# A Mamba block and an FP4 feed-forward on one core: the first tiles of the feed-forward are loaded, quantized and scheduled in another order

## The chip, the core and the metric

The kernel runs on one core of a Trainium2 chip. Its engines are TensorE (PE, with its weight loads shown as PEld), VectorE (DVE), ScalarE (ACT), GpSimd (POOL) and SyncE (SP, which here issues the DMAs). Each engine takes its own instructions in order, and waits on semaphores for the others. The metric is the time of one execution on the device, in microseconds (us). All data are float32.

## What is computed

The input is x with 8192 rows of 512. The first half is a Mamba block; the second a gated feed-forward network (FFN) whose three products take inputs and weights rounded to FP4 in blocks of 16. Cut to what matters:

```python
def fp4_quant_dequant(x):               # along the last dim, BLOCK = 16
    xb = x.reshape(shape[:-1] + (shape[-1] // BLOCK, BLOCK))
    scale = jnp.maximum(jnp.max(jnp.abs(xb), -1, keepdims=True) / 6.0, 1e-12)
    xn = xb / scale
    idx = jnp.searchsorted(_MID, jnp.abs(xn))
    return (_GRID[idx] * jnp.sign(xn) * scale).reshape(shape)
...
gate = fp4_linear(x, w_gate); y = fp4_linear(x, w_up)
h = jax.nn.silu(gate) * y
return fp4_linear(h, w_down)
...
h = _layernorm(x) * (1 + ca) + sa
x = x + ga * mamba(h, ...)
h = _layernorm(x) * (1 + cb) + sb
return x + gb * ffn(h, w_gate, w_up, w_down)
```

The inner width of the FFN is 1408. ga and gb are gates of 512 values, worked out in the kernel from the conditioning vector; gb multiplies the FFN's result column by column.

## The kernel before, in words

The first half works through the 8192 rows in 16 chunks of 512 and writes x's update, gated, to `mo` in DRAM, one tensor per chunk. Its instructions stand in an order written out by hand (`TABLE`, under `tc.manual_schedule()`). Beside its first chunk it quantizes w_gate and w_up and stores them turned in DRAM (`wqs`), and it stores the rows cb+1, sb and gb in `rows`. Its last steps are: the last scan steps (L497) and product with C (L521) on DVE, sums through PE (L392), the gate `z` times y (L404, DVE), four transposes (L410) with copies on ACT (L417), and for each of the last four groups of 128 rows an output projection of eight matmuls (L423), copied from PSUM by ACT (L436, one PSUM buffer) and stored to `mo` (L437).

At `order.close()` the hand-written order ends. From there a scheduler orders the instructions of each engine by data and estimated cost; where it puts one is seen only in the built program. What stands in the code there, in this order: loads of `sb`, `cb1` and the quantized w_gate and w_up (`wg`, `wu`, six loads, L869); `normed` for tile 0 in a pool `hd`; and the last steps of the first half.

The FFN works through 64 tiles of 128 rows:

- `head(t)` calls `normed` (L871 on): it loads `x1` (from `mo`, L874) and `h2` (from x, L876), adds them on POOL (L877), takes the layer norm on DVE (L25 to L32, with a power on POOL, L31), multiplies by cb1 and adds sb on POOL (L879, L880), and quantizes to `xq`.
- `up(t)` transposes xq on PE (L913), copies it (ACT, L937), and in chunks of 512, 512 and 384 columns multiplies it by wg and wu (L945: `pg` and `pu`, two PSUM buffers each), takes silu on ACT (L950) and the product on DVE (L951) into `h`. Then it quantizes h, 1408 wide, to `hq`.
- `down(t)` transposes hq, copies it (ACT, L958), multiplies by `wd` (L962: 11 steps into `po2`), adds to x1 on DVE (L965) and stores the result.

Quantizing, in `_fp4_steps`, is one chain for any width: block maximum (L63, DVE), scale (L65), reciprocal (L67), division `xn` (L69, on the engine given as `first`), magnitude and a slope on ACT (L73, L75), four roundings on DVE (L79 to L82), and the scale put back on POOL (L87).

W_down is quantized in the first four passes, one group of 128 rows per pass, by `quantize_down`, with L69 on DVE; in the pass after, `turn_down` transposes it on PE (L913, shared PSUM buffers `ptp`, two of them), and DVE multiplies the result by gb while it copies it from PSUM (L924). No `down` can run before all of `wd` is there, so `up` runs ahead:

```python
late.append((t, xt, up(t, q)))
if t < NK:
    rows_d[t] = quantize_down(t)
if 0 < t <= NK:
    turn_down(t - 1, rows_d.pop(t - 1))
if t >= NK:
    for _ in range(min(2, len(late) - 1)):
        down(*late.pop(0))
```

NK is 4. Passes 4 to 6 do two down() each, later ones one, and one is left for the end.

Of the kernel before, what the change touches and what calls it, by code (L numbers as in the profile page):

```python
# [8 lines left out]
F32 = mybir.dt.float32  # L9
U32 = mybir.dt.uint32  # L10
AF = mybir.ActivationFunctionType
ALU = mybir.AluOpType
# [4 lines left out]
P = 128  # L17
# [24 lines left out]
    nc.vector.scalar_tensor_tensor(out, sgn, mul, mag, ALU.subtract, ALU.mult)  # L42


def _fp4_steps(nc, work, small, src, dst, n, slope0, first):

    nb = n // BLK
    blocks = lambda t: t.rearrange("p (b k) -> p b k", k=BLK)
    spread = lambda t: t.unsqueeze(2).to_broadcast([P, nb, BLK])
    magic = float(2**21 + 1)
    t = {}

    def scales():
        am = small.tile([P, nb], F32, tag="am", name="am")
        nc.vector.tensor_reduce(am, blocks(src), AX.X, ALU.max, apply_absolute_value=True)  # L63
        sc = t["sc"] = small.tile([P, nb], F32, tag="sc", name="sc")
        nc.vector.tensor_scalar(sc, am, 1.0 / 6.0, 1e-12, ALU.mult, ALU.max)  # L65
        rs = small.tile([P, nb], F32, tag="rs", name="rs")
        nc.vector.reciprocal(rs, sc)  # L67
        xn = t["xn"] = work.tile([P, n], F32, tag="xn", name="xn")
        first.tensor_tensor(blocks(xn), blocks(src), spread(rs), ALU.mult)  # L69

    def leads():
        a = t["a"] = work.tile([P, n], F32, tag="a", name="a")
        nc.scalar.activation(a, t["xn"], AF.Abs)  # L73
        e = t["e"] = work.tile([P, n], F32, tag="e", name="e")
        nc.scalar.activation(e, a, AF.Identity, bias=slope0, scale=2.2)  # L75

    def rounds():
        a, e, xn = t.pop("a"), t.pop("e"), t["xn"]
        nc.vector.scalar_tensor_tensor(e, a, 2.0, e, ALU.add, ALU.max)  # L79
        nc.vector.tensor_scalar(e.bitcast(U32), e.bitcast(U32), 0xFFE00000, None, ALU.bitwise_and)  # L80
        nc.vector.scalar_tensor_tensor(xn, e, magic, xn, ALU.mult, ALU.add)
        nc.vector.scalar_tensor_tensor(xn, e, -magic, xn, ALU.mult, ALU.add)  # L82

    def values():
        xn = t.pop("xn")
        to = xn if dst is None else dst
        nc.gpsimd.tensor_tensor(blocks(to), blocks(xn), spread(t.pop("sc")), ALU.mult)  # L87
        return to

    return scales, leads, rounds, values  # L90


def _fp4(*args):
    for step in _fp4_steps(*args):
        step()
# [3 lines left out]
def mamba_then_fp4_ffn(  # L99
# [18 lines left out]
    nc = tc.nc  # L118
    L, DM = x.shape
    DI = w_outT.shape[0]  # L120
    FF = w_gate.shape[0]
    NS = a_log.shape[2]
    RK = w_dtT.shape[0]
    NK = DM // P
    ND = DI // P
    NF = FF // P
# [10 lines left out]
    small = ctx.enter_context(tc.tile_pool(name="small", bufs=4))  # L137
# [7 lines left out]
    slope0 = glob.tile([P, 1], F32, tag="slope0", name="slope0")  # L145
    nc.gpsimd.memset(slope0, -1.72)
    sc = glob.tile([P, NK], F32, tag="silu_c", name="silu_c")
# [7 lines left out]
    rows = dram.tile([3, DM], F32, tag="rows", name="rows")  # L155


    with ExitStack() as ma:
# [697 lines left out]
                        run(slot, moment)  # L856

        order.close()
        wq = ctx.enter_context(tc.tile_pool(name="wq", bufs=1, side="right", **own))
        wg = wq.tile([P, NK, FF], F32, tag="wg", name="wg")  # L860
        wu = wq.tile([P, NK, FF], F32, tag="wu", name="wu")
# [2 lines left out]
        NCH = [(o, min(512, FF - o)) for o in range(0, FF, 512)]  # L864
        nc.sync.dma_start(sb, rows[0:1, :].partition_broadcast(P))
        nc.sync.dma_start(cb1, rows[1:2, :].partition_broadcast(P))
        for o, w in NCH:
            for t, key in ((wg, "g"), (wu, "u")):
                nc.sync.dma_start(t[:, :, o : o + w], wqs[key][:, :, o : o + w])  # L869

        def normed(t, io, work, small_work, dst):  # L871

            xt = io.tile([P, DM], F32, tag="x1", name=f"x1_{t}")
# [9 lines left out]
                step()  # L883
            return xt, values()


        hd = ctx.enter_context(tc.tile_pool(name="hd", bufs=1, side="right", **own))
        nxt = normed(0, hd, hd, hd, None)

        for slot in range(NSLOT, last + 1):  # L890
            run_all(slot)
# [2 lines left out]
    with ExitStack() as fa:  # L894
        wq2 = fa.enter_context(tc.tile_pool(name="wq2", bufs=1, **own))
        wd = wq2.tile([P, NF, DM], F32, tag="wd", name="wd")
        gb = wq2.tile([P, DM], F32, tag="gb", name="gb")
        nc.sync.dma_start(gb, rows[2:3, :].partition_broadcast(P))
        wide = fa.enter_context(tc.tile_pool(name="wide", bufs=2, **own))
        work = fa.enter_context(tc.tile_pool(name="fwork", bufs=2, **own))  # L900
        fsm = fa.enter_context(tc.tile_pool(name="fsm", bufs=3, **own))
        io = fa.enter_context(tc.tile_pool(name="fio", bufs=NK + 1, **own))
        pdn = fa.enter_context(tc.tile_pool(name="pdn", bufs=2, space=PSUM, **own))
        pgu = fa.enter_context(tc.tile_pool(name="pgu", bufs=2, space=PSUM, **own))
        ptp = fa.enter_context(tc.tile_pool(name="ptp", bufs=2, space=PSUM, **own))

        def transposed(src, nblk, put):

            for b0 in range(0, nblk, 4):
                nb = min(4, nblk - b0)  # L910
                pt = ptp.tile([P, 4, P], F32, tag="mm", name="pt")
                for b in range(nb):
                    nc.tensor.transpose(pt[:, b, :], src[:, (b0 + b) * P : (b0 + b + 1) * P], ident)  # L913
                put(b0, nb, pt)

        def quantize_down(r):
            raw = wide.tile([P, FF], F32, tag="wraw", name=f"wraw_{r}")
            nc.sync.dma_start(raw, w_down[r * P : (r + 1) * P, :])
            _fp4(nc, work, fsm, raw, raw, FF, slope0, nc.vector)
            return raw  # L920

        def turn_down(r, q):

            transposed(q, NF, lambda b0, nb, pt: nc.vector.tensor_tensor(  # L924
                wd[:, b0 : b0 + nb, r * P : (r + 1) * P], pt[:, :nb, :],
                gb[:, r * P : (r + 1) * P].unsqueeze(1).to_broadcast([P, nb, P]), ALU.mult))

        NT = L // P

        def head(t):  # L930
            q = work.tile([P, DM], F32, tag="xq", name=f"xq_{t}")
            return normed(t, io, work, fsm, q)

        def up(t, q):

            qT = work.tile([P, NK, P], F32, tag="xqT", name=f"xqT_{t}")
            transposed(q, NK, lambda b0, nb, pt: nc.scalar.activation(  # L937
                qT[:, b0 : b0 + nb, :], pt[:, :nb, :], AF.Copy))
            hb = wide.tile([P, FF], F32, tag="h", name=f"h_{t}")
            for o, w in NCH:  # L940
                pg = pgu.tile([P, 512], F32, tag="pg", name=f"pg_{t}_{o}")
                pu = pgu.tile([P, 512], F32, tag="pu", name=f"pu_{t}_{o}")
                for ps, wt in ((pg, wg), (pu, wu)):
                    for k in range(NK):
                        nc.tensor.matmul(  # L945
                            ps[:, :w], lhsT=qT[:, k, :], rhs=wt[:, k, o : o + w],
                            start=(k == 0), stop=(k == NK - 1),
                        )
                g = wide.tile([P, 512], F32, tag="g", name=f"g_{t}_{o}")
                nc.scalar.activation(g[:, :w], pg[:, :w], AF.Silu)  # L950
                nc.vector.tensor_tensor(hb[:, o : o + w], g[:, :w], pu[:, :w], ALU.mult)  # L951
            hq = wide.tile([P, FF], F32, tag="q", name=f"hq_{t}", bufs=NK + 1)
            _fp4(nc, work, fsm, hb, hq, FF, slope0, nc.vector)
            return hq

        def down(t, xt, hq):
            hT = wide.tile([P, NF, P], F32, tag="hqT", name=f"hqT_{t}")
            transposed(hq, NF, lambda b0, nb, pt: nc.scalar.activation(  # L958
                hT[:, b0 : b0 + nb, :], pt[:, :nb, :], AF.Copy))
            po = pdn.tile([P, DM], F32, tag="po", name=f"po2_{t}")  # L960
            for f in range(NF):
                nc.tensor.matmul(  # L962
                    po, lhsT=hT[:, f, :], rhs=wd[:, f, :], start=(f == 0), stop=(f == NF - 1)
                )
            nc.vector.tensor_tensor(xt, xt, po, ALU.add)  # L965
            nc.sync.dma_start(out[t * P : (t + 1) * P, :], xt)


        late, rows_d = [], {}
        for t in range(NT):  # L970
            xt, q = nxt
            if t + 1 < NT:
                nxt = head(t + 1)
            late.append((t, xt, up(t, q)))
            if t < NK:
                rows_d[t] = quantize_down(t)
            if 0 < t <= NK:
                turn_down(t - 1, rows_d.pop(t - 1))
            if t >= NK:
                for _ in range(min(2, len(late) - 1)):  # L980
                    down(*late.pop(0))
        for args in late:
            down(*args)


# [38 lines left out]
```

## Time and profile before

Three executions took 6126.43, 6127.5 and 6128.48 us (median 6127.5). The profiled one took 6128.15 us; its span, from the first instruction to the last, is 6126.4 us.

| engine | busy us | share of the span | busy, 4400 to 4430.5 us |
|---|---|---|---|
| PE | 5440.3 | 89% | 29.56 |
| DVE | 4928.0 | 80% | 18.47 |
| POOL | 4147.2 | 68% | 8.33 |
| ACT | 3092.8 | 50% | 7.26 |

The last column is one pass of the settled FFN. The first half ends, and the FFN begins, at about 4040 us of the span. How to read the profile: a group or a stretch says what an engine was doing; "idle before <-X" says how long it stood before an instruction, and what it waited for last. A wait counts against the time only if nothing else is late too. So times of a stage are compared with that stage's own rows, not with averages over the whole span. DVE or POOL being idle costs nothing by itself; PE being idle while it has most of the work does.

### The profile page before, as it was taken

To read this page: it belongs to the slowest core of one execution; us is meant where nothing else is said; L and a number is where in the kernel's file an instruction comes from. 1 tells how busy PE (TensorE), PEld (TensorE's weight loads), DVE (VectorE), ACT (ScalarE), POOL (GpSimd) and SP (SyncE) were. 2 spreads that over 40 slices of the span, in tenths; PEclk is the share of its full clock that TensorE was granted. 3 is DMA by queue.
4 is the path that set the end of the run, shared out by engine and by line. 5 is a ranking of instruction groups with operands and counts; after the bars stand their busy time and mean duration, and the time that the engine had idled before them with its cause. 6 is when DMAs were issued, how large, how long until landed. Compare 5 with 4: busy or idle time off the path is not lost.

```text
span 6126.4 us, 60004 instructions
## 1 busy us (share of the span) xinstructions
PE 5440.3 (89%) x20772; PEld 3253.4 (53%) x20772; DVE 4928.0 (80%) x5007; ACT 3092.8 (50%) x5708; POOL 4147.2 (68%) x2415
## 2 busy tenths in 40 slices
PE   7788888889888888898888888678999999999999
PEld 4555555555555555555555555534444444444444
DVE  6999899999999999999998989966566666666664
ACT  6576666676666666666666665522222222222222
POOL 4999999999999999999989999942222222222221
PEclk9899989889899999898998999888999999999999
DMA  5444444444444444444444444420000000000000
GB/s 179 158 148 148 145 149 150 147 147 146 149 153 144 150 146 148 150 149 150 149 145 148 149 144 149 153 96 24 26 26 25 26 26 26 26 26 23 26 24 14
DMA packets 220552, 659.78 MB, mean 108 GB/s; under 512 B 24371, under 2 KB 36787, under 8 KB 220246
## 3 DMA queue, kind: packets, MB, share of 16 engines
q1 hardware_dynamic: 220246, 655.94, 33.2%
q8 instruction: 163, 2.67, 0.2%
q14 instruction: 143, 1.17, 0.1%
HBM read 615.48 MB, written 40.38 MB: 107 GB/s over the span
## 4 chain that ended last, share of the span: by engine, by line
PE 34%; DVE 19%; ACT 8%; issue 2%; POOL 2%; DVEq 0%; POOLq 0%; DMA 0%; SPq 0%; ACTq 0%
PE pg L945 10%; PE po L962 10%; DVE da L497 10%; PE pu L945 9%; DVE hc L521 4%; ACT da L471 4%; DVE hp L497 3%; PE pt L913 1%; PE cv L296 1%; POOL db L461 1%; PE y L392 1%; ACT xqT L937 1%; ACT L347 1%; PE cv L268 1%; ACT hqT L958 1%
## 5 line engine op out<-in xcount | busy, mean ns | idle before, releaser
L461 POOL TENSOR_TENSOR db<-bc,du 128x1024 f32<-128x1024 f32 x1024 | 2398.0, 2362 | 49.2 <-DVE da L497 41.6
L497 DVE TENSOR_TENSOR_SCAN da<-da,state,db 128x512 f32<-128x512 f32 x1280 | 1645.1, 1285 | 97.4 <-ACT da L471 71.8
L471 ACT ACTIVATE da<-delta,na 128x512 f32<-128x512 f32 x2048 | 1410.6, 690 | 418.5 <-DVE hc L521 197.3
L87 POOL TENSOR_TENSOR hq<-xn,sc 128x1408 f32<-128x1408 f32 x64 | 189.2, 2957 | 1318.3 <-DVE xn L82 1318.3
L497 DVE TENSOR_TENSOR_SCAN hp<-da,state,db 128x512 f32<-128x512 f32 x768 | 941.2, 1267 | 152.1 <-PE y L392 58.5
L392 PE MATMUL y<-ident,hc 128*128 128x128 f32 x5120 | 774.9, 302 | 233.9 <-DVE hc L521 233.7
L513 POOL TENSOR_TENSOR hp<-hp,bc 128x1024 f32<-128x1024 f32 x384 | 904.8, 2356 | 30.8 <-POOL state L512 0.2
L392 PEld LDWEIGHTS y<-ident,hc 128*128 128x128 f32 x5120 | 659.8, 156 | 407.7 <-DVE hc L521 320.2
L521 DVE TENSOR_TENSOR hc<-da,bc 128x1024 f32<-128x1024 f32 x640 | 781.1, 1220 | 30.8 <-DVE da L497 0.9
L945 PE MATMUL pg<-wg,xqT 128*128 128x512 f32 (+1 forms) x1536 | 652.7, 568 | 44.0 <-ACT xqT L937 44.0
L945 PE MATMUL pu<-wu,xqT 128*128 128x512 f32 (+1 forms) x1536 | 635.9, 557 | 0.0
L962 PE MATMUL po<-wd,hqT 128*128 128x512 f32 x1408 | 616.5, 593 | 0.0
L950 ACT ACTIVATE g<-pg 128x512 f32<-128x512 f32 (+1 forms) x192 | 107.8, 561 | 956.9 <-PE pg L945 956.9
L268 PE MATMUL cv<-hT,w_in 128*128 128x512 f32 x1024 | 504.8, 639 | 46.5 <-ACT delta L347 43.2
L296 PE MATMUL cv<-raw,taps 128*128 128x512 f32 x1024 | 523.3, 659 | 6.7 <-ACT taps L282 6.7
L366 PE MATMUL pz<-w_in,hT 128*128 128x256 f32 x2048 | 495.1, 397 | 28.8 <-ACT delta L347 26.4
L945 PEld LDWEIGHTS pg<-wg,xqT 128*128 128x128 f32 x1536 | 290.5, 192 | 361.9 <-issue 250.8
L951 DVE TENSOR_TENSOR h<-g,pu 128x512 f32<-128x512 f32 (+1 forms) x192 | 123.4, 643 | 426.2 <-PE pu L945 421.3
L423 PE MATMUL po<-w_o,xc 128*128 128x512 f32 x1024 | 461.2, 594 | 2.8 <-ACT po L436 2.1
L945 PEld LDWEIGHTS pu<-wu,xqT 128*128 128x128 f32 x1536 | 291.8, 190 | 312.9 <-issue 244.3
L366 PEld LDWEIGHTS pz<-w_in,hT 128*128 128x128 f32 x2048 | 401.3, 201 | 91.7 <-ACT delta L347 32.3
L392 PE MATMUL y<-ident,hp 128*128 128x128 f32 x3072 | 433.6, 288 | 0.0
(118 smaller groups left out, 6347.3 us busy)
## 6 DMA issues: line engine op xcount, KB each, us to landing
bc<-bc SPq DMA_DIRECT2D x1024, 512.0 KB, 4.6
x<-in_x_dram SPq DMA_DIRECT2D x64, 256.0 KB, 4.9
mo<-po SPq DMA_DIRECT2D x64, 256.0 KB, 2.1
h<-in_x_dram SPq DMA_DIRECT2D x64, 256.0 KB, 2.7
x<-mo SPq DMA_DIRECT2D x64, 256.0 KB, 2.6
out_dram<-x SPq DMA_DIRECT2D x64, 256.0 KB, 2.0
w_in<-in_w_inT_dram SPq DMA_DIRECT2D x2, 2048.0 KB, 9.0
wm<-in_wmod_dram SPq DMA_DIRECT2D x8, 512.0 KB, 4.7
```

What stands on the lines that cost most here:

```text
L268: nc.tensor.matmul(ps, lhsT=w_in[:, f, o : o + P], rhs=hT[k][:, f, :], start=(f == 0), stop=(f == NK - 1),)
L296: nc.tensor.matmul(v, lhsT=taps[:, i, :], rhs=raw[:, i : i + T], start=(i == 0), stop=(i == 3))
L366: nc.tensor.matmul(pz[:, b, :], lhsT=hT[k][:, f, t0 : t0 + P], rhs=w_in[:, f, o : o + DH * P], start=(b == 0 and f == 0), stop=(f == NK - ...
L392: nc.tensor.matmul(y[:, j, i * P : (i + 1) * P], lhsT=src[:, j * P : (j + 1) * P], rhs=ident, start=start and j % 2 == 0, stop=stop, is_tr ...
L423: nc.tensor.matmul(pend["po", k, j], lhsT=xcs[k, d][:, j * P : (j + 1) * P], rhs=w_o[:, d, :], start=(d == 0), stop=(d == ND - 1),)
L461: nc.gpsimd.tensor_tensor(db, bct[slot // DH, 0], dus[k, h, i].unsqueeze(1).to_broadcast([P, GN, T]), ALU.mult)
L471: nc.scalar.activation(pend["da", slot][:, q, :], deltas[k, h][:, i, :], AF.Exp, scale=na[:, d, n : n + 1])
L497: nc.vector.tensor_tensor_scan(to[:, q, :], da[:, q, :], db[:, q, :], state[:, d, n : n + 1], ALU.mult, ALU.add,)
L513: nc.gpsimd.tensor_tensor(to, to, c_rows, ALU.mult)
L521: nc.vector.tensor_tensor(hc, hs, c_rows, ALU.mult)
L945: nc.tensor.matmul(ps[:, :w], lhsT=qT[:, k, :], rhs=wt[:, k, o : o + w], start=(k == 0), stop=(k == NK - 1),)
L962: nc.tensor.matmul(po, lhsT=hT[:, f, :], rhs=wd[:, f, :], start=(f == 0), stop=(f == NF - 1))
```

## The change

It changes the start of the FFN in three ways.

- The pool `hd` is opened, and tile 0's `normed` stands, ahead of the six loads of `wg` and `wu` instead of behind them.
- W_down: the division L69 goes to POOL (`first` is `nc.gpsimd`). The gate gb is no longer multiplied in at `turn_down`: it comes as four values per partition (`gc`, one load of 4-byte pieces), each group of 128 rows has its own column of it, and after the reciprocal the scales `sc` are multiplied by that (one short DVE instruction of 88 elements), so that L87 puts scale and gate in together. `turn_down` is then a plain copy on ACT.
- h is kept unquantized (`hbp`, four buffers) and quantized later, by a new function `quantized`: from pass 3 on, after the passes' down(), for at most one tile in pass 3 and two in later ones; those are taken by down() in the pass after. `hq` has two buffers instead of five, and x1 has six instead of five.

```diff
-def _fp4_steps(nc, work, small, src, dst, n, slope0, first):
+def _fp4_steps(nc, work, small, src, dst, n, slope0, first, mul=None):
...
         nc.vector.reciprocal(rs, sc)
+        if mul is not None:
+            nc.vector.tensor_scalar(sc, sc, mul, None, ALU.mult)
...
         order.close()
+        hd = ctx.enter_context(tc.tile_pool(name="hd", bufs=1, side="right", **own))
...
-        for o, w in NCH:
-            for t, key in ((wg, "g"), (wu, "u")):
-                nc.sync.dma_start(t[:, :, o : o + w], wqs[key][:, :, o : o + w])
...
-        hd = ctx.enter_context(tc.tile_pool(name="hd", bufs=1, side="right", **own))
         nxt = normed(0, hd, hd, hd, None)
+        for o, w in NCH:
+            for t, key in ((wg, "g"), (wu, "u")):
+                nc.sync.dma_start(t[:, :, o : o + w], wqs[key][:, :, o : o + w])
...
-        gb = wq2.tile([P, DM], F32, tag="gb", name="gb")
-        nc.sync.dma_start(gb, rows[2:3, :].partition_broadcast(P))
+        gc = wq2.tile([P, NK], F32, tag="gc", name="gc")
+        nc.sync.dma_start(gc, rows[2:3, :].rearrange("o (r p) -> p (o r)", p=P))
+        hbp = fa.enter_context(tc.tile_pool(name="hbp", bufs=NK, **own))
-        io = fa.enter_context(tc.tile_pool(name="fio", bufs=NK + 1, **own))
+        io = fa.enter_context(tc.tile_pool(name="fio", bufs=NK + 2, **own))
...
-            _fp4(nc, work, fsm, raw, raw, FF, slope0, nc.vector)
+            _fp4(nc, work, fsm, raw, raw, FF, slope0, nc.gpsimd, gc[:, r : r + 1])
...
-            transposed(q, NF, lambda b0, nb, pt: nc.vector.tensor_tensor(
-                wd[:, b0 : b0 + nb, r * P : (r + 1) * P], pt[:, :nb, :],
-                gb[:, r * P : (r + 1) * P].unsqueeze(1).to_broadcast([P, nb, P]), ALU.mult))
+            transposed(q, NF, lambda b0, nb, pt: nc.scalar.activation(
+                wd[:, b0 : b0 + nb, r * P : (r + 1) * P], pt[:, :nb, :], AF.Copy))
...
-            hb = wide.tile([P, FF], F32, tag="h", name=f"h_{t}")
+            hb = hbp.tile([P, FF], F32, tag="h", name=f"h_{t}")
...
-            hq = wide.tile([P, FF], F32, tag="q", name=f"hq_{t}", bufs=NK + 1)
+            return hb
+
+        def quantized(t, hb):
+            hq = wide.tile([P, FF], F32, tag="q", name=f"hq_{t}")
             _fp4(nc, work, fsm, hb, hq, FF, slope0, nc.vector)
             return hq
...
-            if t >= NK:
-                for _ in range(min(2, len(late) - 1)):
-                    down(*late.pop(0))
-        for args in late:
-            down(*args)
+            finish()
+            for _ in range(min(2, len(late), max(0, t - NK + 2))):
+                n, xt, hb = late.pop(0)
+                ready.append((n, xt, quantized(n, hb)))
+        finish()
```

`finish()` calls down() for all that is in `ready` and empties it. In the built program the change orders SP's queue after the last loads of the first half so: x1 and h2 of tiles 0 to 2, x1 of tiles 3 to 6, sb, cb1, the six weight loads, then the stores of `mo`, `gc` and W_down's loads. Before, h2 of tiles 1 and 2, sb, cb1 and the weights came first, then x1 and h2 of tile 0. On DVE, the first steps of tile 0's layer norm stand ahead of the last L521 and of L404 in the changed kernel, behind them in the kernel before; on ACT, the two L73 and two L75 of tiles 0 and 1 stand ahead of the first L436, behind the third before; on PE, the transposes of tile 0 stand between the second and third projection, and one of its matmuls ahead of the fourth. On POOL, L69 of a group of W_down stands behind L87 of the group before.

More of the change, by code (lines that the diff above doesn't have):

```diff
@@ L966, in down, with finish @@
             nc.sync.dma_start(out[t * P : (t + 1) * P, :], xt)
-        late, rows_d = [], {}
+        late, ready, rows_d = [], [], {}
+        def finish():
+            for args in ready:
+                down(*args)
+            ready.clear()
         for t in range(NT):
```

## The prediction

> **What bounds the kernel now.** I read the page's forty slices first, then the busy times of stretches about the hand-over to the FFN, then the waits there, then each engine's order of time.
>
> ```profile
> PE   7788888889888888898888888678999999999999
> DVE  6999899999999999999998989966566666666664
> ```
>
> A slice is 153 us. From slice 28 on, PE is full and nobody else is; before slice 26 it shares with DVE. The change touches only what lies between: the end of the first half and the first FFN tiles. Stretches (columns: stretch, length, busy PE, PEld, DVE, ACT, POOL, clock, DMA share, GB/s):
>
> ```profile
> 4072.00:4109.00 37.00, 23.44 (x66) 11.90 (x64) 36.80 (x39) 12.22 (x13) 8.55 (x4) 0.83 0.05 11
> 4109.00:4149.00 40.00, 24.26 (x64) 12.26 (x65) 33.89 (x43) 11.02 (x13) 14.91 (x10) 0.76 0.11 40
> 4149.00:4183.00 34.00, 24.51 (x64) 12.16 (x65) 29.86 (x31) 9.07 (x11) 7.16 (x3) 0.80 0.03 8
> 4233.00:4275.00 42.00, 41.40 (x119) 20.48 (x120) 19.74 (x28) 9.69 (x16) 11.17 (x10) 1.00 0.10 31
> ```
>
> Three passes of up() take 34 to 40 us with DVE 85 to 99% busy and PE waiting; from 4233 PE has no gap. So only about 4008 to 4233 can be won. Who waits there (total, times, longest):
>
> ```profile
> POOL x L877 <- DMA h<-in_x_dram: 23.7, 2, 22.4
> PE pt L913 <- DVE wd L924: 30.0, 8, 7.7
> PE pt L913 <- POOL wraw L87: 6.7, 1, 6.7
> PE pt L913 <- POOL xn L87: 4.9, 1, 4.9
> ```
>
> And PE in order of time:
>
> ```profile
> 4036.41 7.13 PE L423 MATMUL po<-w_o,xc 128*128 128x512 f32 x16 [0.69 <-ACT po L436]
> 4048.41 1.07 PE L913 MATMUL pt<-ident,xn 128*128 128x128 f32 x4 [4.87 <-POOL xn L87]
> 4098.89 1.97 PE L913 MATMUL pt<-ident,wraw 128*128 128x128 f32 x8 [6.73 <-POOL wraw L87]
> 4106.36 0.90 PE L913 MATMUL pt<-ident,wraw 128*128 128x128 f32 x3 [5.50 <-DVE wd L924]
> 4146.29 1.09 PE L913 MATMUL pt<-ident,xq 128*128 128x128 f32 x4 [7.26 <-DVE wd L924]
> 4148.72 6.47 PE L945 MATMUL pg<-wg,xqT 128*128 128x512 f32 x8 [1.35 <-ACT xqT L937]
> 4155.03 3.60 PE L945 MATMUL pu<-wu,xqT 128*128 128x512 f32 x8
> ```
>
> PE stands while DVE empties the transposes of W_down (L924) between long quantizations; then its first matmuls run slow (6.47 for 3.60). The gate matmuls of tiles 1 to 6 begin at 4073.0, 4109.4, 4148.7, 4182.7, 4233.1, 4274.7.
>
> **What the skill says.** *GPSIMD Engine Reference*, Specifications: GpSimd's way into SBUF is shared with VectorE, in contention when DVE reads two SBUF inputs or runs in a two-port mode. The trace agrees:
>
> ```profile
> 4154.54 3.17 POOL L87 TENSOR_TENSOR hq<-xn,sc 128x1408 f32<-128x1408 f32 x1 [14.85 <-DVE xn L82]
> 4155.30 3.89 DVE L81 SCALAR_TENSOR_TENSOR xn<-e,xn 128x1408 f32<-128x1408 f32 x1
> ```
>
> L81 takes 1.6 alone; here it ends 1.5 after POOL. So I let L32, L65, L69, L79 to L82 and POOL's tensor operations exclude each other; L63, L25, L951 (PSUM) don't. Same page, Engine selection: two-input work is some twice slower on GpSimd; here L69 is 1.61 for 1408 on DVE and 2.02 for 1024 on POOL, so 2.77 for 1408 as an estimate. *TensorE: Matmul & The Clock Gate*, Part 1: half clock after an idle window of about 3.4 us; the 6.47 agrees.
>
> **The change part by part.** I wrote out the queues with the rows' durations and followed each wait. For the kernel before this puts tile 4 at 4182.8 (trace 4182.7) and tile 6 at 4272.4 (4274.7), so the method is good to some 2 us.
>
> *Loads of the first tiles.* x1_0 is issued when the last db is done (4002.3), seven x1 and three h loads and sb, cb1 ahead of the weights, 0.35 each; two land in 2.6. The weights start at 4012 for 4007.7 and, moving at 0.33 MB/us as before, are there by 4030; needed at 4043. But work for tiles 0 to 2 now stands in DVE's queue ahead of the last hc (L521) and z (L404): bn_stats of tile 0 waits for the add (4005.4 + 1.27), and L32 for rstd, behind three adds on POOL. z goes from 4009.0 to 4012, the projections start 2.4 later. Next, POOL's six L879/L880 of three tiles (7.6) end at 4023; L69 follows, then four activations (2.7), and only behind these stands ACT's copy of the first projection, at 4026.3: PE waits 4.6 instead of 0.7 (+3.9), and goes cold (+2.7). The last projection ends near 4052 for 4043.5. up(0) follows without the old 4.87 + 0.69, one matmul already done: 4052 + 18.0 (18.9 of matmuls less 0.86) = 4070.0 for 4071.7, and tile 1 starts at 4070.8: gain 2.2. Ahead of the weights the early tile buys little: what it saves, the projections lose.
>
> *W_down and the moved quantization, passes 1 to 3.* DVE did per pass: three L951 1.9, quantize h 9.8 (1.61+0.20+0.69+1.61+1.62+0.88+1.62+1.61), W_down 9.8, three L924 1.9, next tile 5.9: 29.3, plus standing for POOL. The first 9.8 goes to later passes, L924 to ACT (0.60, 0.60, 0.49; ACT 25 to 35% busy), L69 to POOL; the sc multiply adds 0.2. Left: 16.2. POOL holds the port 2.77 twice, 1.06 and three times 1.27 = 10.4, of which DVE stands perhaps 7: 23 against PE's 20.6 (18.9 and 15 transposes of 0.11). So PE is nearly fed, once it runs. At first it isn't: W_down 0 comes at 4058, since SP holds it behind the last mo's landing and gc; POOL divides 4063.2 to 4066, ACT 2.9, DVE's steps for it and tile 2 to 4079, L87 to 4081.8; W_down 1's division stands in POOL's queue behind that, so its L87 ends at 4102.1, and its transposes stand ahead of tile 2's matmuls. PE, done at 4091, waits 10.2. Tile 2 at 4103 (36.4 becomes 32.2, gain 4.2). Then waits of 0.5 to 0.9 stand in for 6.74+7.26+1.35 and 0.45+7.69+1.35, with clock: tile 3 at 4127 (39.3 becomes 24.1, gain 15.2), tile 4 at 4148.6 (33.9 becomes 21.5, gain 12.4). Sum 34.0.
>
> *What comes back.* Quantizations of h now fall in passes 3 to 6, two a pass; with W_down 3 and tile heads DVE is full from 4130 to 4198. ACT's wd copies stand behind an activation that waits for DVE: 6.4 before the first po, 4.7 before tile 5, both cold. Tile 4 to 5: before 50.4 with two down() of 11.05, so 28.3 without; after 45.4 with one, 34.3: loss 6.0. Tile 5 to 6: 41.6 becomes 44.1, loss 2.5. The down() still owed comes in pass 7; it is no loss. Net 34.0 - 8.5 = 25.5. As my order of the kernel before was 2.3 short, some of its unlisted idling will be in the new one too: I take 24.
>
> *At no price.* After tile 8 each pass keeps its order but for L877 and the x1 load a step earlier; PE covers that (31.4 a pass, DVE 18.5, POOL 8.3 of 30.5). Without this cover it would be 1.3 a pass. The tail (5.92 for the last hq) is the same. gc is 512 pieces of 4 bytes, which no row shows: *DMA: Bandwidth & Descriptors*, Specifications, puts pieces under 512 bytes off line rate; between cc (128 pieces: 0.39 to issue, 1.6 to land) and wg (512 pieces, 5.6 to land), I take 2; its landing is needed only at 4066, its issue delays W_down one for one. POOL's division: 2.2 gives 27 in all, 3.4 gives 20.
>
> Profiled: 6128.15 (span 6126.4 and 1.75 around) - 24 = 6104.1; the median was 0.65 below it: **6103.5**.
>
> **Rivals.** *Feeding better than I count* (DVE not stopped by POOL's division, W_down 1 not late): the 10.2, 6.4 and 4.7 shrink; without that stop 4 more us, with all of the gaps gone 21 more: 6082 to 6099. For: POOL waits often here; against: L81's 3.89. *The hand-over is worse*: twelve loads at once land late, and z, projections and up(0) shift with them. From 2 us of lateness on each us is one lost; h landed in up to 9.2 in the trace behind the weights, so 4 to 12 late: gain 22 to 14, and with a cold clock on top inside 0.2%: 6106 to 6120. *It turns slower*: gc's 4-byte pieces hold SP, with both first W_down loads behind it, before anything is on wd. Price one for one, deciding from 24 us; 40 would give 6143. Against: cc's 0.39, and bdt, dsk of 4 KB land in under 5. *The early load does nothing* is what I forecast of that part already.
>
> **Numbers.** Mine (6097 to 6110) 0.62; better fed 0.14; hand-over worse 0.20, half of it within 0.2% (12.3 us, about what a measurement of this kernel can tell from no change); slower 0.04. Faster by over 0.2% is 0.62 + 0.14 + 0.10 = 0.86, within 0.10, slower 0.04. Range 6092 to 6117: it leaves out the upper end of the hand-over case and most of the gap-free one.
>
> **What would show it.** z near 4012; an ACT copy of the first po after four activations; tile 1 at 4071; about 10 us idle before W_down 1's transposes; no PE wait above 2 us in passes 2 and 3; DVE dense to 4198; waits of 4 to 7 at tiles 4 and 5; passes of 31.4 afterwards. Wrong, if POOL's 1408 division is far from 2.77, if gc issues slowly, or if later passes aren't 31.4.

## The result, and the profile after

| | before | after |
|---|---|---|
| median, us (lowest to highest of 6 runs each) | 6126.97 (6126.11 to 6128.48) | 6099.02 (6098.02 to 6100.32) |
| the profiled execution: time / span | 6128.15 / 6126.4 | 6098.98 / 6097.2 |

The ratio is 0.9954, with a 95% interval of 0.9941 to 0.9967: 27.95 us faster. 24 was forecast, and 6099.0 lies in the range.

In the changed kernel's profile lines 69 to 85 are what was 67 to 82, the scale put back is L90 (L87), z L407 (L404), the projection L426 (L423) and its copy L439 (L436), transposes L916 (L913), the wd copy L927 (L924), gate and up matmuls L947 (L945), h L953 (L951). Its forty slices end the weak stretch of PE one slice (153 us) earlier: slices 25 to 28, counted from 1, were 8, 6, 7, 8 and are 7, 7, 7, 9 (so before the change PE's first full slice was the 29th, not the 28th). Such a slice is too long to show more:

```profile
PE   7788888888888888898888887779999999999999
DVE  7999899989998999999999999967566666666664
```

Four stretches of it (length; busy PE, PEld, DVE, ACT, POOL; clock; DMA share; GB/s). PE is nearly full in the second and third, which are passes 2 and 3 (98 and 95%, where those passes had 61 and 72% before); in the fourth DVE is full and PE is not:

```profile
4072.00:4103.00 31.00, 21.18 (x64) 11.04 (x63) 23.44 (x28) 8.10 (x12) 16.41 (x11) 0.82 0.10 33
4103.00:4127.00 24.00, 23.41 (x67) 11.64 (x66) 19.18 (x24) 7.73 (x11) 10.40 (x8) 0.95 0.14 41
4127.00:4149.00 22.00, 20.86 (x61) 10.46 (x60) 22.00 (x22) 8.74 (x10) 5.44 (x4) 1.00 0.00 1
4149.00:4194.00 45.00, 34.49 (x98) 17.86 (x98) 43.95 (x44) 16.71 (x21) 14.78 (x6) 0.89 0.06 18
```

What PE waited for between 4000 and 4240 (total, times, longest). The 30.0 behind L924 are gone; three single waits are left:

```profile
PE pt L916 <- POOL wraw L90: 9.5, 1, 9.5
PE pt L916 <- ACT wd L927: 7.3, 4, 6.1
PE pg L947 <- ACT xqT L939: 7.0, 4, 4.4
```

The same in PE's order of time:

```profile
4015.41 9.41 PE L426 MATMUL po<-w_o,xc 128*128 128x512 f32 x16 [0.75 <-ACT xc L420]
4025.73 7.13 PE L426 MATMUL po<-w_o,xc 128*128 128x512 f32 x16 [0.90 <-ACT po L439]
...
4068.43 3.70 PE L947 MATMUL pg<-wg,xqT 128*128 128x512 f32 x8 [1.68 <-ACT xqT L939]
...
4099.46 1.11 PE L916 MATMUL pt<-ident,wraw 128*128 128x128 f32 x4 [9.53 <-POOL wraw L90]
...
4172.31 0.90 PE L916 MATMUL pt<-ident,wraw 128*128 128x128 f32 x3 [6.14 <-ACT wd L927]
...
4191.09 5.19 PE L947 MATMUL pg<-wg,xqT 128*128 128x512 f32 x8 [4.36 <-ACT xqT L939]
```

The last but one hc step of the scan (L521, now L524) begins at 4002.77 in the profile before and at 4001.61 in that after; nothing that PE or DVE does has changed by then. So stage times are counted from that step from here on: "tile 1 at 66.8" is the begin of tile 1's gate matmuls, 66.8 us after it. Forecast and measurement, the forecast times less 4002.77:

| | before | forecast | after |
|---|---|---|---|
| z | 6.3 | 9.2 | 9.2 |
| last projection ends | 40.8 | 49.2 | 46.9 |
| tile 1 | 70.2 | 68.0 | 66.8 |
| tile 2 | 106.6 | 100.2 | 98.8 |
| tile 3 | 146.0 | 124.2 | 122.8 |
| tile 4 | 179.9 | 145.8 | 144.5 |
| tile 5 | 230.3 (two down() before it) | 191.2 (one) | 189.5 (one) |

### The profile page after: what moved, and what is told of

It reads as the page before. It is cut to its first block, busy times and chain, and to the rows that moved or that the text cites. A ratio compares the mean times of both kernels' runs of the same rounds, so it can differ in the third digit from the quotient of the medians.

```text
span 6097.2 us, 60081 instructions
## 1 busy us (share of the span) xinstructions
PE 5406.6 (89%) x20772; PEld 3232.6 (53%) x20772; DVE 4933.1 (81%) x4995; ACT 3097.9 (51%) x5720; POOL 4222.9 (69%) x2419
## 5 line engine op out<-in xcount | busy, mean ns | idle before, releaser
L395 PE MATMUL y<-ident,hc 128*128 128x128 f32 x5120 | 761.7, 299 | 249.5 <-DVE hc L524 246.6
L524 DVE TENSOR_TENSOR hc<-da,bc 128x1024 f32<-128x1024 f32 x640 | 781.3, 1221 | 30.8 <-DVE da L500 0.9
L878 POOL TENSOR_TENSOR x<-x,h 128x512 f32<-128x512 f32 x64 | 148.9, 2327 | 808.1 <-DMA h<-in_x_dram 692.9
L947 PE MATMUL pg<-wg,xqT 128*128 128x512 f32 (+1 forms) x1536 | 646.5, 564 | 45.3 <-ACT xqT L939 45.3
L947 PE MATMUL pu<-wu,xqT 128*128 128x512 f32 (+1 forms) x1536 | 635.9, 557 | 0.0
L271 PE MATMUL cv<-hT,w_in 128*128 128x512 f32 x1024 | 506.7, 641 | 48.5 <-ACT delta L350 45.2
L369 PE MATMUL pz<-w_in,hT 128*128 128x256 f32 x2048 | 494.6, 397 | 35.3 <-ACT delta L350 32.9
L90 POOL TENSOR_TENSOR hq<-xn,sc 128x1408 f32<-128x1408 f32 x64 | 183.9, 2873 | 473.7 <-DVE xn L85 392.9
L953 DVE TENSOR_TENSOR h<-g,pu 128x512 f32<-128x512 f32 (+1 forms) x192 | 123.1, 641 | 470.2 <-PE pu L947 460.4
L947 PEld LDWEIGHTS pg<-wg,xqT 128*128 128x128 f32 x1536 | 288.3, 191 | 358.7 <-issue 247.8
L426 PE MATMUL po<-w_o,xc 128*128 128x512 f32 x1024 | 463.5, 596 | 1.7 <-ACT po L439 0.9
L947 PEld LDWEIGHTS pu<-wu,xqT 128*128 128x128 f32 x1536 | 291.8, 190 | 312.7 <-issue 231.5
```

Source lines behind the costliest of these rows:

```text
L271: nc.tensor.matmul(ps, lhsT=w_in[:, f, o : o + P], rhs=hT[k][:, f, :], start=(f == 0), stop=(f == NK - 1),)
L369: nc.tensor.matmul(pz[:, b, :], lhsT=hT[k][:, f, t0 : t0 + P], rhs=w_in[:, f, o : o + DH * P], start=(b == 0 and f == 0), stop=(f == NK - ...
L395: nc.tensor.matmul(y[:, j, i * P : (i + 1) * P], lhsT=src[:, j * P : (j + 1) * P], rhs=ident, start=start and j % 2 == 0, stop=stop, is_tr ...
L426: nc.tensor.matmul(pend["po", k, j], lhsT=xcs[k, d][:, j * P : (j + 1) * P], rhs=w_o[:, d, :], start=(d == 0), stop=(d == ND - 1),)
L524: nc.vector.tensor_tensor(hc, hs, c_rows, ALU.mult)
L947: nc.tensor.matmul(ps[:, :w], lhsT=qT[:, k, :], rhs=wt[:, k, o : o + w], start=(k == 0), stop=(k == NK - 1),)
```

## The experiments

What had to be told apart: which of the three parts makes the gain, and whether what comes back in passes 4 to 6 comes from DVE's load, from GpSimd's division, or from the order on ACT. Each median is of 5 or more runs and stands beside the kernel before on the same chip (6126.7 to 6127.3); the interval is that of the ratio to it. In the profiled executions the hc step begins between 4000.2 and 4002.8, whatever the edit, so a difference of 2 or 3 us between medians is to be read beside the stage times.

| run | median us | 95% interval | tile 1 | tile 2 | tile 4 | tile 5 |
|---|---|---|---|---|---|---|
| early_only | 6120.3 | 0.9982 to 0.9995 | 65.0 | 101.3 | 173.8 | 223.7 |
| wdown_only (with the early load) | 6116.0 | 0.9975 to 0.9989 | 65.9 | 104.5 | 171.0 | 217.5 |
| late_quant_only (with the early load) | 6092.4 | 0.9931 to 0.9956 | 66.1 | 96.7 | 150.8 | 185.8 |
| late_quant_old_pool | 6084.8 | 0.9918 to 0.9945 | 70.6 | 94.5 | 143.4 | 178.7 |
| after_no_early | 6098.1 | 0.9940 to 0.9965 | 66.5 | 98.3 | 144.0 | 188.8 |
| after_old_pool | 6094.1 | 0.9935 to 0.9960 | 67.9 | 93.8 | 139.7 | 184.5 |
| after_early_behind_z | 6096.3 | 0.9938 to 0.9963 | 64.9 | 96.8 | 142.4 | 187.2 |
| after_div_dve | 6087.6 | 0.9924 to 0.9949 | 66.3 | 94.4 | 140.1 | 181.6 |
| after_gate_dve | 6092.6 | 0.9931 to 0.9956 | 65.8 | 95.6 | 149.2 | 185.2 |
| div_dve_old_pool | 6087.0 | 0.9921 to 0.9948 | 67.9 | 91.2 | 137.8 | 178.7 |
| after_one_a_pass | 6104.5 | 0.9951 to 0.9976 | 66.4 | 98.2 | 147.1 | 188.0 |
| all_three | 6095.6 | 0.9935 to 0.9962 | 64.5 | 92.2 | 140.7 | 178.5 |

### The parts alone

**early_only**, from the kernel before:

```diff
+        hd = ctx.enter_context(tc.tile_pool(name="hd", bufs=1, side="right", **own))
         wq = ctx.enter_context(tc.tile_pool(name="wq", bufs=1, side="right", **own))
...
-        for o, w in NCH:
-            for t, key in ((wg, "g"), (wu, "u")):
-                nc.sync.dma_start(t[:, :, o : o + w], wqs[key][:, :, o : o + w])
...
-        hd = ctx.enter_context(tc.tile_pool(name="hd", bufs=1, side="right", **own))
         nxt = normed(0, hd, hd, hd, None)
+        for o, w in NCH:
+            for t, key in ((wg, "g"), (wu, "u")):
+                nc.sync.dma_start(t[:, :, o : o + w], wqs[key][:, :, o : o + w])
```

> The kernel before with one part of the change: pool hd and tile 0's normed ahead of the six weight loads; W_down and the quantization of h as before. Theory (the gain comes from the vector work taken out of passes 1 to 3, the early load buys about 2 us or nothing): within 4 us of before, either sign (6123 to 6131). Rival A (the early load brings the gain, as it ends the 22.4 us wait for h and the 4.87 wait of tile 0's transposes): 15 us or more faster, 6112 or less.

Measured: 7 us faster, more than the theory and less than rival A. Tile 1 comes 5.3 earlier, and passes 1 and 2, which DVE bounds, are as long as before (36.4 and 39.4).

**late_quant_only**, from the changed kernel:

```diff
-        gc = wq2.tile([P, NK], F32, tag="gc", name="gc")
-        nc.sync.dma_start(gc, rows[2:3, :].rearrange("o (r p) -> p (o r)", p=P))
+        gb = wq2.tile([P, DM], F32, tag="gb", name="gb")
+        nc.sync.dma_start(gb, rows[2:3, :].partition_broadcast(P))
...
-            _fp4(nc, work, fsm, raw, raw, FF, slope0, nc.gpsimd, gc[:, r : r + 1])
+            _fp4(nc, work, fsm, raw, raw, FF, slope0, nc.vector)
...
-            transposed(q, NF, lambda b0, nb, pt: nc.scalar.activation(
-                wd[:, b0 : b0 + nb, r * P : (r + 1) * P], pt[:, :nb, :], AF.Copy))
+            transposed(q, NF, lambda b0, nb, pt: nc.vector.tensor_tensor(
+                wd[:, b0 : b0 + nb, r * P : (r + 1) * P], pt[:, :nb, :],
+                gb[:, r * P : (r + 1) * P].unsqueeze(1).to_broadcast([P, nb, P]), ALU.mult))
```

with the weight loads put ahead of `normed` again in the code, but `hd` left where the change puts it.

> The kernel before with one part of the change: h kept in four buffers and quantized later, one tile in pass 3 and two a pass from then on; W_down's division, its gate on DVE and the order of the first loads as before. Theory (9.8 us of DVE work leaves each of passes 0 to 2; what is left, 19.5 and what it stands for POOL, is near PE's 20.6): most of the gain, 15 to 24 us faster, 6103 to 6112; the gap at the first transposes of W_down 1 gets shorter than 9.5, as its division doesn't stand in POOL's queue. Rival B (DVE still holds the transposes through the gate multiplication, so the quantization alone buys little): 0 to 8 faster, 6119 to 6127.

Measured: 6092.4, better than the theory gave, and 6.6 below the changed kernel itself. "The order of the first loads as before" was not so: its SP queue had tile 0's loads first, as in the change. It holds the early load, without W_down's part.

**wdown_only**, from the kernel before: the `mul` argument, `gc`, `nc.gpsimd` and the copy on ACT of the change; `hd` was in its new place here too.

> The kernel before with one part of the change: W_down's division on GpSimd, the gate in its row scales (loaded as gc), the copy of its transposes on ACT; quantization of h and the first loads as before. Theory (DVE keeps 29.3 - 3.5 of its work a pass and stands longer for POOL, so passes 1 to 3 stay bound by DVE at 27 to 32 us): 3 to 12 us faster, 6115 to 6124. Rival B (it was the gate multiplication on DVE that kept PE standing): 15 or more faster, 6112 or less. Rival C (POOL's 1408-wide division stops DVE and queues behind L87, and costs more than it spares): slower than before, 6128 or more.

Measured: 6116.0, as the theory has it, but 7 of the 11 us are the early load's: beside early_only W_down's part is worth 4.3. Put on top of late_quant_only it costs 6.6.

**late_quant_old_pool**, from late_quant_only:

```diff
-        hd = ctx.enter_context(tc.tile_pool(name="hd", bufs=1, side="right", **own))
         wq = ctx.enter_context(tc.tile_pool(name="wq", bufs=1, side="right", **own))
...
+        hd = ctx.enter_context(tc.tile_pool(name="hd", bufs=1, side="right", **own))
         nxt = normed(0, hd, hd, hd, None)
```

> As late_quant_only, but with pool hd opened behind the weights' pool again, as in the kernel before: in late_quant_only the SP queue still had tile 0's loads ahead of the weights, since it was the pool's place and not the place in the code that moved them. Theory (the delayed quantization alone is worth most, the early tile 0 on top of it 2 to 7 us as in early_only): 6093 to 6100. Rival A (the early tile 0 is needed for it): 6104 or more.

Measured: 6084.8, under the lower end. The delayed quantization alone makes 42 us; the other two parts of the change give 14 of them back. This is the fastest of all the kernels run.

### The early load inside the change

**after_no_early** is the changed kernel with the weight loads put back ahead of `normed`; `hd` stays:

```diff
+        for o, w in NCH:
+            for t, key in ((wg, "g"), (wu, "u")):
+                nc.sync.dma_start(t[:, :, o : o + w], wqs[key][:, :, o : o + w])
         def normed(t, io, work, small_work, dst):
...
         nxt = normed(0, hd, hd, hd, None)
-        for o, w in NCH:
-            for t, key in ((wg, "g"), (wu, "u")):
-                nc.sync.dma_start(t[:, :, o : o + w], wqs[key][:, :, o : o + w])
```

> The changed kernel with its weight loads put back ahead of tile 0's normed. Theory: as the changed kernel, within 4 us (6095 to 6103), since what the early tile saves, the scan end and the projections lose. Rival A (the early load is needed, since a tile 0 that waits for h 22 us shifts all passes): 5 to 12 us slower than the changed kernel, 6104 to 6111.

Measured: 6098.1, no difference. It was no test of the early load: SP's order was the same. With `hd` ahead of `wq`, the place in the code changes nothing there.

**after_old_pool** puts the pool back too (the edit of late_quant_old_pool, on after_no_early).

> The changed kernel with pool hd and tile 0's normed wholly where they were, behind the weights (after_no_early moved back the code only, not the pool). Theory: the early tile 0 saves what it did in early_only, 7 us, or less, where the wait behind W_down 0 hides it: 6099 to 6106. Rival: no effect, 6097 to 6100, as a W_down 0 that comes at the same time sets tile 2's start.

Measured: 4.9 *faster* than the changed kernel. Theory and rival both had the wrong sign. Tile 1 is 1.1 later, tile 2 is 4.9 earlier. SP's queue shows what lies between; in the changed kernel first, W_down's first two loads stand behind the last store of `mo` and gc:

```profile
4041.34 8.19 SPq L440 DMA_DIRECT2D mo<-po  x2
4051.24 0.37 SPq L900 DMA_DIRECT2D gc<-rows  x1
4051.67 0.97 SPq L921 DMA_DIRECT2D wraw<-in_w_down_dram  x2
```

and in after_old_pool:

```profile
4042.65 0.32 SPq L440 DMA_DIRECT2D mo<-po  x1
4044.69 0.37 SPq L900 DMA_DIRECT2D gc<-rows  x1
4045.11 0.98 SPq L921 DMA_DIRECT2D wraw<-in_w_down_dram  x2
```

From the hc step the loads go out at 50.1 and at 43.9, since the last projection ends at 46.9 and at 40.8. W_down 0 and 1 are what DVE has to do here. In the first 67 us after the hc step (length, busy DVE, clock, DMA share, GB/s), the changed kernel:

```profile
4001.61:4068.61 67.00, 32.14 (x56) 0.90 0.50 179
```

and after_old_pool:

```profile
4001.21:4068.21 67.00, 37.44 (x59) 0.95 0.39 141
```

DVE has 5.3 us more behind it, and tile 2 comes 4.9 earlier. In both, tile 2 begins 0.7 to 1 us after POOL has put W_down 1's scale back (L90 ends at 97.8 and 93.1).

**after_early_behind_z** has tile 0's `normed` ahead of the weights in the code, but `hd` opened behind `wq`:

```diff
-        hd = ctx.enter_context(tc.tile_pool(name="hd", bufs=1, side="right", **own))
         wq = ctx.enter_context(tc.tile_pool(name="wq", bufs=1, side="right", **own))
...
+        hd = ctx.enter_context(tc.tile_pool(name="hd", bufs=1, side="right", **own))
         nxt = normed(0, hd, hd, hd, None)
         for o, w in NCH:
```

> The changed kernel with pool hd opened behind the weights' pool as before, but tile 0's normed still ahead of the weights in the code. In its built program x1 and h2 of tile 0 stand right ahead of the weight loads on SP, and the last scan product and z stand ahead of tile 0's layer norm on DVE, as in the kernel before. Theory (what the early load loses is z and the projections, held by DVE's layer norm ahead of them, not the loads): z 6.25 after the last but one hc step as before, not 9.20, the last projection 40.8 after it, not 46.9, tile 1 at 62 to 65, not 66.8, and 3 to 9 us faster than the changed kernel, 6090 to 6096. Rival (the twelve loads at once are what costs, or it doesn't count as W_down 0 and 1 come when they come): 6096 to 6101.

Measured: 2.7 faster than the changed kernel, short of the theory's 3 and at the rival's edge; tile 6 begins only 1.1 earlier (231.4 for 232.6). z is back at 6.3 and tile 1 at 64.9, as the theory has it. The last projection is not: 45.3 for 40.8. PE's order shows why:

```profile
4029.06 0.80 PE L916 MATMUL pt<-ident,xn 128*128 128x128 f32 x4 [3.16 <-POOL xn L90]
4029.65 8.63 PE L426 MATMUL po<-w_o,xc 128*128 128x512 f32 x16
```

Tile 0's transposes stand ahead of the third projection and wait for xn. So mo's last store and W_down's loads are late again (48.5), and pass 1 takes 31.9, as in the changed kernel, where after_old_pool has 26.0. With z in time, tile 1 comes 1.9 earlier than in the changed kernel; a pass 1 of 26.0 would be worth 5.9. So a late z is the smaller part of what the early load costs. That the larger one is W_down's loads behind the last store is argued from these times: no run moves those loads alone.

What holds W_down 0's load there is gc. Both loads stand behind it on SP, and SP waits at gc for the landing of a store of `mo` (total, times, longest):

```profile
SPq L900 <- DMA mo<-po: 1.6, 1, 1.6
```

In late_quant_only, which loads `gb` in its place, SP has the same wait at `gb`, but behind both loads, and W_down 0's goes out ahead of the last store:

```profile
4041.24 0.32 SPq L440 DMA_DIRECT2D mo<-po  x1
4041.61 0.42 SPq L921 DMA_DIRECT2D wraw<-in_w_down_dram  x1
4049.11 0.32 SPq L440 DMA_DIRECT2D mo<-po  x1
```

From the hc step W_down 0's load goes out at 40.4 there (40.1 in after_gate_dve, below), and at 50.1 with gc. What these 10 us are worth by themselves was not measured.

### W_down's part taken apart

**after_div_dve**:

```diff
-            _fp4(nc, work, fsm, raw, raw, FF, slope0, nc.gpsimd, gc[:, r : r + 1])
+            _fp4(nc, work, fsm, raw, raw, FF, slope0, nc.vector, gc[:, r : r + 1])
```

> The changed kernel with one part undone: W_down's division back on DVE, the gate still in the row scales and the copy still on ACT. Theory 1 (POOL's queue, with W_down 1's division behind W_down 0's last step, and DVE standing behind POOL's division are what costs): about as late_quant_only or better, 6085 to 6093, with the gap ahead of W_down 1's transposes well under 9.5. Theory 2 (the wd copies on ACT, and what they make the scheduler do with ACT's order at tile 5, are what costs): as the changed kernel, 6096 to 6101. Theory 3 (passes 4 to 6 are DVE's, so each DVE instruction added comes on top): 6100 to 6106.

Measured: 6087.6, 11.5 below the changed kernel: theory 1. The gap ahead of W_down 1's transposes is 5.6 for 9.5, and no pass is slower. The row of the short multiplication of the scales (least, median and longest ns, first and last start, form) in the changed kernel:

```profile
L70 DVE TENSOR_SCALAR sc<-sc,gc x4: 246/2424/2602, 4061.1 to 4131.3; 128x88 f32<-128x88 f32 x4
```

and in after_div_dve:

```profile
L70 DVE TENSOR_SCALAR sc<-sc,gc x4: 165/172/267, 4059.7 to 4124.6; 128x88 f32<-128x88 f32 x4
L72 DVE TENSOR_TENSOR xn<-wraw,rs x4: 1617/1618/2095, 4059.8 to 4126.4; 128x1408 f32<-128x1408 f32 x4
```

In three of four groups DVE stands at an instruction of 88 elements per partition until POOL's division is done. In the changed kernel POOL's row and DVE's say it together:

```profile
4061.03 2.59 POOL L72 TENSOR_TENSOR xn<-wraw,rs 128x1408 f32<-128x1408 f32 x1 [17.95 <-DVE rs L68]
```

```profile
4061.08 2.60 DVE L70 TENSOR_SCALAR sc<-sc,gc 128x88 f32<-128x88 f32 x1
```

To have a measure of all such standing, I took, for each DVE instruction listed alone in the 185 us after the hc step, what it took over the short ones of its form: some 24 us in the changed kernel, 11 to 12 in after_div_dve. The division would cost DVE 4 x 1.62 = 6.5; on POOL it spares that and costs 12. The net of 6 is close to tile 5's 7.9. The other half of theory 1, the place of W_down 1's division in POOL's queue, differs little between the two: on POOL that division begins 79.0 after the hc step, on DVE 76.6.

**after_gate_dve**, with `gb` loaded and multiplied in at `turn_down` on DVE as in the diff of late_quant_only, and the division left on GpSimd:

```diff
-            _fp4(nc, work, fsm, raw, raw, FF, slope0, nc.gpsimd, gc[:, r : r + 1])
+            _fp4(nc, work, fsm, raw, raw, FF, slope0, nc.gpsimd)
```

> The changed kernel with the other part undone: W_down's division on GpSimd, the gate multiplied in on DVE while it copies the transposes from PSUM, as before. Theory 1 (POOL's division costs): as the changed kernel or slower, 6097 to 6106. Theory 2 (the ACT copies cost): about as late_quant_only, 6088 to 6094.

Measured: 6092.6, theory 2's figure, although theory 1 had just been met. Both hold in part, and they don't add: the one undone is worth 11.5, the other 6.4, both 6.6 (late_quant_only). But this edit undoes more than the ACT copy: the short multiplication L70 is gone, and with `gb` for gc W_down 0's load goes out 10 us earlier. DVE's standing, by the measure above, is hardly less without L70 (some 23 us), so it seems to fall on other instructions; the earlier load is not separated from the ACT copy. By stage the ACT copy is a gain first and a loss later: passes 2 and 3 take 53.5 with the gate on DVE, 45.8 with it on ACT; pass 4 takes 36.1 and 45.0. In pass 4 ACT's copy stands behind L76, an activation that waits for DVE's division of h. It still does with the division of W_down on DVE (after_div_dve), where PE waits 6.5 for it:

```profile
4166.44 1.38 ACT L76 ACTIVATE a<-xn 128x1408 f32<-128x1408 f32 x1 [5.47 <-DVE xn L72]
4167.72 0.47 ACT L927 ACTIVATE wd<-pt 128x384 f32<-128x384 f32 x1
```

**div_dve_old_pool** is after_old_pool with the edit of after_div_dve.

> The changed kernel with tile 0 wholly as before (as in after_old_pool) and W_down's division on DVE (as in after_div_dve), two late quantizations a pass as in the change. After_old_pool was 4.9 and after_div_dve 11.5 us below the changed kernel. If these are separate, 6081 to 6084 and faster than late_quant_old_pool's 6084.8. If both end at one limit (DVE's work with what it stands for POOL sets when tile 5 begins, 178 to 182 us after the last but one hc step, in every version), 6085 to 6089.

Measured: 6087.0, the case of one limit. Tile 5 begins at 178.7, as it does in late_quant_old_pool, which has nothing of W_down's part: with tile 0 loaded as before and the division on DVE, the gate in the scales and the ACT copies bring nothing in all. They bring tile 4 5.6 earlier, and pass 4 gives it back (41.0 for 35.3).

### The quantizations spread out

**after_one_a_pass**:

```diff
-            for _ in range(min(2, len(late), max(0, t - NK + 2))):
+            for _ in range(min(1 if t < 2 * NK - 1 else 2, len(late), max(0, t - NK + 2))):
```

> The changed kernel, with one tile quantized late per pass in passes 3 to 6 and two from pass 7 on, where it has two from pass 4 on; nothing else. Theory (what comes back in passes 4 to 6 is DVE's load there, with ACT's wd copies behind an activation that waits for DVE): tile 4 to 5 falls from 45.0 toward PE's 32 to 36, the waits of 6.1 and 4.4 at the first down() and at tile 5 shrink below 3, and tile 5 to 6 is 31 to 33 with one down() less; 8 to 13 us faster than the changed kernel, 6086 to 6091. Rival (the waits come from the order in which the scheduler put ACT's copies, whatever DVE's load): waits stay, 6096 to 6101.

Measured: 5.4 *slower* than the changed kernel; theory and rival both fail. The waits in passes 4 and 5 do shrink, to 3.7 at the first down() and 0.25 at tile 5, but W_down 3 came later (tile 4 at 147.1), so that tile 5 is only 1.5 earlier. The rest came back where the two a pass now fall:

```profile
4284.27 1.12 PE L916 MATMUL pt<-ident,hq 128*128 128x128 f32 x4 [3.36 <-POOL hq L90]
4347.64 4.54 PE L947 MATMUL pu<-wu,xqT 128*128 128x384 f32 x8 [1.87 <-DVE h L953]
4364.88 0.55 PE L916 MATMUL pt<-ident,hq 128*128 128x128 f32 x3 [1.61 <-ACT hqT L963]
```

The passes there take 34.1, 44.0 and 46.8, where 30.5, 41.6 and 41.6 are PE's own: 11.2 given back. I had counted DVE as free there, since settled passes leave it a third; but in the scheduler's order the h products of the next tile stand behind steps of the extra quantization: in the last of these passes PE waits 1.87 for one although DVE is busy for only 34.2 of 46.8 us. The pass of 44.0 has hardly any waiting; it follows the 3.36, with a granted clock of 0.94.

**all_three** joins after_early_behind_z, after_div_dve and this edit.

> The changed kernel with pool hd behind the weights' pool (as in after_early_behind_z), W_down's division on DVE (as in after_div_dve) and one late quantization per pass until pass 6 (as in after_one_a_pass). If the three causes are separate: 5 + 11 + 10 us less than the changed kernel, 6070 to 6078. If they are one and the same limit (DVE's work until tile 5 with what it stands for POOL), the parts overlap: 6078 to 6087.

Measured: 6095.6, above both cases. Tile 5 is at 178.5, so its start is as good as the best; the spread quantizations lose it again in the passes from 7 on (33.7, 43.4 and 47.8 for the three from tile 7 to tile 10).

## Why the prediction was right, and where it was not

- **Hand-over.** z at 9.2 was right, and so was the time at which ACT's copy comes free (23.5 after the hc step, by forecast and trace). That PE waits 4.6 for it and runs the second projection cold was not. The projections began 3.6 later than before, not 2.4, and the cold clock fell on the first (9.41 for 7.13; the granted clock was 0.50 up to 4020, 1.00 after), so it ended just as the copy came free and only 0.9 of wait was left. The forecast had tied the cold clock to the 4.6 of idling; here no wait of PE in the 15 us before was longer than 2.9. The projections end 2.3 earlier than forecast, and tile 1 1.2.
- **Passes 1 to 3.** 32.2, 24.1 and 21.5 were forecast, 31.9, 24.1 and 21.7 came. The wait of 10.2 ahead of W_down 1's transposes was 9.5, and no PE wait in passes 2 and 3 reaches 2. POOL's division took 2.58 to 2.59 for the estimated 2.77. W_down 0's first step on DVE began 54.8 after the hc step, forecast 55.2.
- **What comes back.** 6.0 and 2.5 were forecast for passes 4 and 5. Measured: 44.95 less one down() of 11.05 is 33.9, against 28.3 before, so 5.6; and 43.1 for 41.6, so 1.5. The waits of 6.1 and 4.4 stood where 6.4 and 4.7 were put, with DVE busy 43.95 of 45.
- **The sum.** The terms come to 3.4 + 4.4 + 15.3 + 12.2 - 5.6 - 1.5 = 28.2. The 1.5 that I took off for idling that my order of the kernel before had missed was not needed. That, 1.2 at the hand-over and 1.4 in passes 4 and 5 are the 4 us by which my gain was too small.
- **Later passes** are 31.4, as forecast. The tail, put at the same, is not: PE waits 6.36 for the last hq, not 5.92, and the last down() takes 10.84, not 10.15. One pass of 30.5 in place of one of 31.4 makes up for most of that; the forecast had neither.
- **gc** was issued in 0.37, landed in 2.6 (2 was the estimate) and was not late for L70, so its small pieces cost nothing that shows. That W_down's first loads stand behind it, which the rival said, is so; they stand there because gc waits for `mo`, and not because it is slow.
- **"Ahead of the weights the early tile buys little"** was right at tile 1 and too kind beyond it. I priced z and the projections. That SP holds W_down 0 behind the last mo and gc I had too, and it is in the 10.2 of pass 1; but I never asked how much of that the early load brings by making the projections late. With tile 0 loaded as before, the changed kernel is 4.9 us faster (after_old_pool). Alone, in passes that DVE bounds, the same load is worth 7.
- **W_down's division.** I put DVE's standing for POOL at "perhaps 7" a pass, and 4 us on being without it, but didn't set that against the 6.5 that the move spares. With the division back on DVE the kernel is 11.5 us faster. The sum was right with the move in it, so a right sum says nothing of whether each part is worth having; that W_down's part feeds PE was right for passes 1 to 3 alone, which is 8 us in passes 2 and 3, all of it owed again by tile 5.

*Trainium Architecture — The Big Picture*, What this means for kernel authors, calls the ports that DVE and GpSimd share "an exclusive lock (not a bandwidth split)". The trace agrees: L70 started 0.05 after POOL's division and ended 0.06 after it.

Open: what fixes tile 5 at 178.7 in two so different kernels. That DVE is full in pass 4 (34.99 of 35.28 us in late_quant_old_pool, 39.55 of 40.96 in div_dve_old_pool) fits a limit by DVE. But in late_quant_old_pool PE is nearly full there too (34.13 of 35.28; 33.90 of 40.96 in the other), so a limit by PE is not ruled out, and the equal figures may be chance. Issuing W_down's loads ahead of gc and mo's last store, by itself, was not tried.

## What to carry to other kernels

Price each part of a change against leaving it out, not only inside the sum: here one of three parts made 42 us, and the other two gave back 14. An operation moved from VectorE to GpSimd costs VectorE whatever it stands for meanwhile, and a two-input one took longer there (2.59 for 1.62) than it spared. When work is moved out of a stage, follow it to where it is owed, and follow an earlier load to the loads that it pushes back on the same queue.

## What the runs showed of the hardware

- A VectorE instruction of 88 elements per partition, 0.17 us by itself, took 2.60 when GpSimd had begun a 1408-wide division 0.05 us before: as long as the whole of it, however short its own need.
- PE's clock was granted at half for the first 128x512 projections (16 took 9.41 for 7.13) with no wait longer than 2.9 us in the 15 us before them.
- Of the build and not of the chip: which loads come first depended on where the pool is opened. With `hd` ahead of `wq`, both orders of the code gave the same order on SP and times within 1 us of each other (6098.1 and 6099.0). With `hd` behind `wq` the place in the code did count: tile 0's loads stood ahead of the weights in after_early_behind_z and behind them in after_old_pool. Why the pool's place does this was not tested.
